# A ring of four pairs of PSUM banks: one pool's choice, or four named buffers in turn

## The chip, the cores and the metric

The kernel runs on one core of one Trainium2 chip. The metric is the device time of one execution in microseconds (us); the kernel before has a median of 836.28 us over 4 runs (833.42 to 839.04). Clock figures are those of TensorE as the profile records them: 1.00 is full speed, 0.50 half.

## The reference

Input x has 4 sequences of 1024 tokens with 256 channels, all in float32. Two residual layers follow each other.

```
x = x + causal_attention(layernorm(x))     # 16 heads of 16, ALiBi slopes, softmax, output projection
x = x + ffn(layernorm(x))                  # below
```

The second layer attends over the 4 sequences at each token position (16 heads, softmax over 4), projects, adds and normalises, and then sends every token to one expert out of 8: the router takes the two best of 8 logits, and the larger index of the two is the expert. The expert is two 256 x 256 matrices with an exact GELU between them; its output is added and normalised again.

## The kernel before

`fast_layer` writes the program out in a fixed order; nothing is reordered afterwards. The attention over 1024 positions is cut into units. A unit is a sequence and a block of queries, 256 of them (units 0 to 11) or 128 (units 12 to 19, the last quarter of the positions). For every unit and each of 4 groups of 4 heads there are rounds over the keys:

- `score` (L950) takes two pairs of PSUM banks (`sk_unit_group_round_0` and `_1`), fills them with matmuls of `slots` with `slots`, lets ScalarE take the exponential of each pair into a `probs` buffer `p` (7 of them), and lets GpSimd cut the diagonal blocks (`affine_select`, L981).
- `weigh` (L987) handles the probabilities two rounds later: it takes one more pair (`pv_unit_group_round`), fills its first bank with matmuls of `p` with the values `v`, and ScalarE or VectorE moves it to `yt`, which goes to DRAM for later normalising (`y<-yt`, L1031).
- Beside these rounds, planned by hand in slots with costs (`E_slot`, `D_slot`), runs everything else: projections of q, k and v (`qkp`, `vp`, copied to `kq` and `v`), the division by the sums of the softmax (`load_sums` L1038, `invert`, `load_y`, `divide`: tiles `sums`, `inverse`, `su`, `yc`), the output projection (`project`, tile `op`, added to `x`), and the second layer's `front` (L1546: `u`, `ut`, `qkvp`, `pr`, `sc`, `ctx`, `ctp`, `ao`, `place`, `rank`).

All of these take their PSUM from one place. PSUM has 8 banks; during the attention all 8 belong to the pool `ps_s` as four pairs. `pair_of_banks` (L658) takes a pair for `score` or `weigh`; `bank` (L662) takes a pair for the other work and gives it out in halves, the second half to the next caller that needs one bank. A second half goes with the pair's name, so in the profile `kq<-op` is a copy out of the second half of a pair whose first half is `op`. A pair is free again when its last reader, a ScalarE or a VectorE instruction, has read it; until then the first matmul into it waits, and all of TensorE's queue behind that matmul.

As each engine executes in order, the time of a wait depends on which pair is next. The pool before is one ring of four buffers under one tag, and the pool chooses which of them a call gets when the program is built. That is nearly always the pair taken four calls ago, and in a few places it is not.

After the attention three single banks (`tail_banks`) and the pool `ps_x` serve the last position block and the expert tiles (`mtp`, `hid`, `oe`), which end with indirect DMAs to the output (L1924).

The engines are called PE (TensorE), PEld (its weight loads), DVE (VectorE), ACT (ScalarE), POOL (GpSimd) and SP (SyncE, which issues most DMAs) in the profile. Nearly all rows have line L584, a helper that records operands, so rows are told apart by their tiles.

Of the kernel before, what the change touches and what calls it, by code (L numbers as in the profile page):

```python
# [29 lines left out]
F32 = mybir.dt.float32  # L30
# [5 lines left out]
PSUM = bass.MemoryType.PSUM  # L36

P = 128
# [6 lines left out]
QC = 512  # L45
# [557 lines left out]
def fast_layer(ctx: ExitStack, tc: tile.TileContext, odd, x, wq, wk, wv, wp, w_in, w_out, w_r,  # L603
# [27 lines left out]
    pool = lambda name, bufs, **k: tc.tile_pool(name=name, bufs=bufs, **k)  # L631
# [7 lines left out]
    attention = ExitStack()  # L639
    pad = attention.enter_context(pool("pad", 1))  # L640
    act = attention.enter_context(pool("act", 1))
    probs = attention.enter_context(pool("probs", N_PROBS))
    ps_s = attention.enter_context(pool("ps_s", 4, space=PSUM))

    def const(name, shape, dtype=F32, into=keep):
        return into.tile(shape, dtype, tag=name, name=name)
# [5 lines left out]

    half_of = []
    tail_banks = []

    def pair_of_banks(name):  # L658
        half_of.clear()
        return ps_s.tile([P, 2, QC], F32, tag="s", name=name)  # L660

    def bank(name):  # L662
        if tail_banks:
            return tail_banks[0].tile([P, QC], F32, tag="m", name=name)
        if half_of:
            return half_of.pop()
        pair = pair_of_banks(name)
        halves[pair.tensor.name] = [], []
        half_of.append(pair[:, 1])
        return pair[:, 0]  # L670
# [279 lines left out]
    def score(u, g, r):  # L950
# [4 lines left out]
        qt = slots[g][:, i * P:(i + size) * P]  # L955
        own = r == n_rounds(u) - 1
        ps = [pair_of_banks(f"sk_{name}_{k}") for k in range(2)]
        width = 0
        for kb, off in blocks_of(u, r):
# [27 lines left out]
    def weigh(rounds_):  # L987
# [4 lines left out]
        for u, g, r, pts in rounds_:  # L992
            if not parts or parts[-1][0] != (u, g):
                parts.append(((u, g), []))
            parts[-1][1].append((r, pts))
        pm = pair_of_banks("pv_{}_{}_{}".format(*rounds_[0][:3]))[:, 0]
        for k, ((u, g), of_part) in enumerate(parts):
            n, i, size = units[u]
# [1325 lines left out]
@with_exitstack  # L2324
def tile_layer(ctx: ExitStack, tc: tile.TileContext, *args):
    nc = tc.nc
    flag = ctx.enter_context(tc.tile_pool(name="flag", bufs=1))
    odd = flag.tile([P, 1], I32, tag="odd", name="odd")
    fast_layer(tc, odd, *args)
    again = nc.values_load(  # L2330
        odd[0:1, 0:1], min_val=0, max_val=1,
        skip_runtime_bounds_check_because="a comparison's result",
    )
    with tc.If(again > 0):
        general_layer(tc, *args)
# [75 lines left out]
```

## Time and profile before

| | us |
|---|---|
| median of 4 runs | 836.28 (833.42 to 839.04) |
| the profiled execution, its own time | 833.63 |
| its span, first to last instruction | 831.9 |
| PE busy | 724.7 (87%) |
| DVE busy | 547.0 (66%) |
| ACT busy | 417.6 (50%) |
| POOL busy | 255.3 (31%) |
| mean granted clock | 0.943 |

The stages by the clock of the span: about 100 us of preparation and first units, attention with the second layer's fronts beside it to about 655 us, the last front and the first expert tiles to about 740 us, then expert tiles to the end. In a timeline row the columns are start, busy time, engine, line, operation, out<-in, shapes, count, and in brackets the idle time before it with what ended it. `pv<-p,v x64` is 64 matmuls of one shape, merged.

### The profile page before, as it was taken

Reading aid. Unit: us, or ns where it says so; the run is one execution under the profiler, and the core shown is the slowest. Engines: PE = TensorE matmul, PEld = TensorE weight load, DVE = VectorE, ACT = ScalarE, POOL = GpSimd, SP = SyncE. Lnnn points to the kernel's source line nnn. Section 1 sums busy time; section 2 is a strip of 40 time slices with the busy share of each in tenths; the row PEclk is TensorE's granted clock in tenths of the full one; section 3 lists DMA queues with packets and bytes.
Section 4 is the critical chain, followed back from the end, with each engine's and each line's share of the span. In section 5 each row is a group of like instructions: output and inputs, shape, how many; then the busy total and the mean of one; then the engine's idle time right before and its main releaser. Section 6 shows DMA issues by size and latency. Waiting matters only on the chain. (4 is left out here: it accounts for less than half of the span.)

```text
span 831.9 us, 22499 instructions
## 1 busy us (share of the span) xinstructions
PE 724.7 (87%) x8917; PEld 542.8 (65%) x8917; DVE 547.0 (66%) x1316; ACT 417.6 (50%) x625; POOL 255.3 (31%) x360
## 2 busy tenths in 40 slices
PE   4987989999899889999989997988988799878972
PEld 2765667666566556665668876767766567767772
DVE  7245336429647957595778748388479779885663
ACT  1554446666455636665456456557445345333540
POOL 5433113212111301121122112112112414648885
PEclk9798989999999989999989999999998899898996
DMA  7444454434522415152444535424421662233430
GB/s 216 118 128 143 130 159 126 144 110 132 153 73 76 126 47 171 54 164 72 123 124 144 149 108 146 126 78 126 145 78 28 208 231 77 71 108 120 128 100 24
DMA packets 75219, 99.56 MB, mean 120 GB/s; under 512 B 19496, under 2 KB 58723, under 8 KB 74596
## 3 DMA queue, kind: packets, MB, share of 16 engines
q1 hardware_dynamic: 64576, 79.63, 32.4%
q0 software_dynamic: 4864, 14.16, 5.6%
q10 hardware_dynamic: 5668, 4.25, 1.7%
q8 instruction: 73, 1.20, 0.6%
q14 instruction: 38, 0.31, 0.1%
HBM read 61.55 MB, written 35.12 MB: 116 GB/s over the span
## 5 line engine op out<-in xcount | busy, mean ns | idle before, releaser
L584 ACT ACTIVATE p<-sk 128x1024 f32<-128x1024 f32 (+1 forms) x320 | 288.4, 939 | 180.1 <-PE sk L584 158.0
L981 POOL TENSOR_SCALAR_AFFINE_SELECT p<-p 128x512 f32<-128x512 f32 (+1 forms) x160 | 106.3, 669 | 447.5 <-ACT p L584 445.1
L584 PE MATMUL sk<-slots 32*128 32x128 f32 (+1 forms) x3456 | 185.7, 332 | 22.6 <-DVE rank L584 6.8
L584 PEld LDWEIGHTS sk<-slots 32*128 32x128 f32 x3456 | 139.7, 191 | 69.6 <-issue 24.5
L584 PE MATMUL pv<-p,v 128*32 128x128 f32 (+1 forms) x3456 | 148.4, 320 | 9.8 <-DVE x L584 3.1
L584 PEld LDWEIGHTS pv<-p,v 128*32 128x32 f32 x3456 | 99.4, 114 | 48.2 <-issue 9.3
L584 PE MATMUL qkvp<-w_in,ut 128*128 128x264 f32 (+1 forms) x236 | 83.2, 486 | 0.0
L584 PEld LDWEIGHTS qkvp<-w_in,ut 128*128 128x128 f32 x236 | 41.2, 190 | 29.1 <-issue 24.8
L584 PE MATMUL oe<-w,ge 128*128 (+1 forms) x152 | 43.8, 413 | 12.9 <-DVE stats_v L584 6.7
L584 DVE COPY qkv<-qkvp 128x264 f32<-128x264 f32 x28 | 12.1, 432 | 61.9 <-PE qkvp L584 61.9
L1808 POOL DMA_INDIRECT given<-rows,rows x38 | 42.8, 1126 | 20.0 <-DVE at_t L584 10.0
L584 PE MATMUL hid<-mt,w 128*128 128x128 f32 x304 | 46.9, 292 | 2.1 <-DMA w<-in_w_dram 1.4
L584 PEld LDWEIGHTS hid<-mt,w 128*128 128x128 f32 x304 | 41.9, 200 | 3.4 <-DMA w<-in_w_dram 1.7
L1924 POOL DMA_INDIRECT out_dram<-o,out_rows x38 | 39.8, 1046 | 8.7 <-issue 5.9
L584 DVE TENSOR_TENSOR pv<-qkv,sc 128x1024 f32<-128x1024 f32 x32 | 40.5, 1267 | 0.3 <-PE ctp L584 0.2
L584 DVE TENSOR_REDUCE sc<-pr 128x64 f32<-128x1024 f32 x32 | 39.0, 1220 | 1.1
L584 DVE TENSOR_TENSOR pr<-qkv 128x1024 f32<-128x1024 f32 x32 | 39.5, 1236 | 0.0
L584 PE MATMUL op<-wp,yc 128*128 128x256 f32 x124 | 33.4, 410 | 7.0 <-issue 3.4
L584 PE MATMUL qkp<-xt,wqk 128*128 128x256 f32 x144 | 38.8, 416 | 0.2 <-ACT p L584 0.2
L584 PEld LDWEIGHTS oe<-w,ge 128*128 128x128 f32 x152 | 27.2, 200 | 17.6 <-DVE given L584 7.5
L584 ACT COPY qkv<-qkvp 128x512 f32<-128x512 f32 (+1 forms) x31 | 17.3, 561 | 40.9 <-PE qkvp L584 40.8
L584 PE MATMUL vp<-wv,xt 128*128 128x256 f32 x128 | 35.0, 421 | 0.0
(320 smaller groups left out, 1053.1 us busy)
## 6 DMA issues: line engine op xcount, KB each, us to landing
slots<-k SPq DMA_DIRECT2D x128, 80.0 KB
k<-kq SPq DMA_DIRECT2D x32, 256.0 KB
v<-v SPq DMA_DIRECT2D x16, 288.0 KB
v<-v SPq DMA_DIRECT2D x4, 1152.0 KB
x<-in_x_dram SPq DMA_DIRECT2D x16, 256.0 KB
y<-yt SPq DMA_DIRECT2D x16, 256.0 KB
rows<-x SPq DMA_DIRECT2D x32, 128.0 KB
slots<-k SPq DMA_DIRECT2D x64, 64.0 KB
```

Of the source, the lines that this page charges most:

```text
L584: ins = made(*args, **kwargs)
L981: nc.gpsimd.affine_select(blocks, blocks, pattern=[[0, 2], [0, size], [1, P]], compare_op=ALU.is_ge, fill=0.0, base=0, channel_multiplier=-1,)
L1808: nc.gpsimd.indirect_dma_start(out=self.hx, out_offset=None, in_=t.rows_of, in_offset=bass.IndirectOffsetOnAxis(ap=t.rows_[:, self.j:self. ...
L1924: ins = nc.gpsimd.indirect_dma_start(out=out.rearrange("t n c -> (t n) c"), out_offset=bass.IndirectOffsetOnAxis(ap=t.table.out_rows[:, t. ...
```

## The change

The pool `ps_s` gets one buffer per tag, and four tags `s0` to `s3`. A counter goes up at each call of `pair_of_banks`, and its remainder by 4 picks the tag. So every call takes the pair that was taken four calls before, whichever was read last.

```diff
-    ps_s = attention.enter_context(pool("ps_s", 4, space=PSUM))
+    ps_s = attention.enter_context(pool("ps_s", 1, space=PSUM))
...
-    half_of = []
+    half_of, n_pairs = [], [0]
     tail_banks = []
 
     def pair_of_banks(name):
         half_of.clear()
-        return ps_s.tile([P, 2, QC], F32, tag="s", name=name)
+        n_pairs[0] += 1
+        return ps_s.tile([P, 2, QC], F32, tag=f"s{n_pairs[0] % 4}", name=name)
```

No computation, shape or order of instructions differs. What differs in the built program is the instruction whose end a TensorE matmul waits for, at six places (the matmul, then the reader of its pair before and after):

```
105 us  pv_4_0_0      turned_w copy (ACT)      -> kq<-op copy (DVE)
        sk_4_2_0_1    kq<-op copy (DVE)        -> p_4_1_1_0 (ACT)
508 us  pv_15_0_0     x<-x,op (DVE)            -> p_15_1_0_1 (ACT)
        sk_15_2_0_0   p_15_1_0_1 (ACT)         -> x<-x,op (DVE)
559 us  sk_17_0_1_1   rank<-place (DVE)        -> p_17_0_0_0 (ACT)
        sk_17_1_0_0   p_17_0_0_1 (ACT)         -> rank<-place (DVE)
567 us  pv_17_0_0     x<-x,op (DVE)            -> p_17_1_0_1 (ACT)
        sk_17_2_0_0   p_17_1_0_1 (ACT)         -> x<-x,op (DVE)
623 us  sk_19_0_1_1   rank<-place (DVE)        -> p_19_0_0_0 (ACT)
        sk_19_1_0_0   p_19_0_0_1 (ACT)         -> rank<-place (DVE)
640 us  pv_19_1_0     yn<-sum (DVE)            -> p_19_2_0_1 (ACT)
        sk_19_3_0_0   p_19_2_0_1 (ACT)         -> yn<-sum (DVE)
```

Three more matmuls beside these (`sk_4_2_0_0`, `pv_16_3_0`, `pv_18_3_0`) change from one ScalarE reader to its neighbour.

## The prediction

> **What bounds the kernel now.** I read the page's busy table and its 40 slices first, then TensorE's waits from 500 to 660 us, then the timeline around each place that the change touches, then a table of stretches for clock and VectorE load. TensorE is busy 724.7 of 831.9 us and fills nearly every slice, so in most of the attention part it sets the time. The list of TensorE's waits (waiting instruction, releaser, total us, times, longest us) shows where it does not:
>
> ```profile
> PE sk L584 <- DVE rank L584: 6.8, 2, 3.4
> PE ctp L584 <- DVE ctx L584: 4.2, 3, 2.0
> PE pv L584 <- DVE x L584: 3.1, 1, 3.1
> PE pv L584 <- DVE yn L584: 2.9, 1, 2.9
> ```
>
> Rows 1, 3 and 4 are waits for a PSUM pair: VectorE's `rank`, `x` and `yn` instructions are no operands of `sk` or `pv`; they are the last readers of the pair that was to be reused. That is 12.75 us in four stalls (3.10, 3.38, 3.38, 2.89). Compared instruction by instruction, the two built programs have the same instructions in the same order on every engine, and differ only in what 15 TensorE instructions wait for. They form six places; in each, two pairs swap their turn, one freed by ScalarE, one by VectorE. Five of the six decide, so each is worked out below. A fifth stall of this kind, at 110.38 us, is made longer.
>
> The second thing to see is what lies beside the stalls. In the table of stretches (us; busy of PE, PEld, DVE, ACT, POOL; granted clock; DMA share; GB/s):
>
> ```profile
> 505.00:508.00 3.00, 0.04 (x4) 0.00 (x0) 2.93 (x8) 1.11 (x2) 0.36 (x1) 0.98 0.85 319
> 508.00:511.30 3.30, 3.15 (x58) 2.58 (x58) 3.16 (x6) 0.81 (x1) 0.31 (x2) 0.50 0.95 291
> 619.60:623.00 3.40, 0.04 (x2) 0.00 (x0) 3.33 (x4) 1.43 (x2) 0.00 (x0) 1.00 0.62 161
> 623.00:627.40 4.40, 4.38 (x90) 3.93 (x92) 4.19 (x10) 2.05 (x2) 1.14 (x2) 0.61 0.01 4
> ```
>
> VectorE is full exactly where TensorE stands still, so a removed stall may only send TensorE to VectorE's next result. And after each such idle time the granted clock is 0.50 for about 3.4 us (0.61 over 4.4 us is 3.4 us at half).
>
> **The price of such a slow spell.** 64 `pv` matmuls take 1.88 us at full clock (566.88 to 568.76), 56 of them take 3.15 at half (508.14 to 511.29), so a factor of 1.92, and a spell of 3.4 us that falls on busy TensorE costs 3.4 x (1 - 1/1.92) = 1.6 us.
>
> ```profile
> 508.14 3.21 PE L584 MATMUL pv<-p,v 128*32 128x128 f32 x56 [3.10 <-DVE x L584]
> ...
> 566.88 1.96 PE L584 MATMUL pv<-p,v 128*32 128x128 f32 x64
> ```
>
> **Part A, unit 4 at 105 us.** Today `pv_4_0_0` takes the pair of `turned_w`, free at 104.86. In strict turn it takes the pair of `op_1`, whose last reader is the copy to `kq`:
>
> ```profile
> 105.03 1.72 PE L584 MATMUL pv<-p,v 128*32 128x256 f32 x32
> 106.68 0.70 PE L584 MATMUL sk<-slots 32*128 32x256 f32 x4
> 109.64 0.68 DVE L584 COPY kq<-op 128x512 f32<-128x512 f32 x1
> 110.38 0.50 PE L584 MATMUL sk<-slots 32*128 32x256 f32 x4 [3.00 <-DVE kq L584]
> ```
>
> The copy is held by `inverse` at the head of VectorE's queue, which waits for the DMA of `sums` until 107.53, so it stays at 110.32. The 3.00 us stall becomes 5.35, and the work that ran ahead of it (pv 1.65, sk 0.70) comes behind it: +2.35. Queued behind the waiting `pv` are all later matmuls, and the exp whose `probs` buffer it frees. The clock now drops only after 111.9; with the idle time from 105.03 on I expect it low already at 110.38, 1.5 us x (1 - 1/1.92) = 0.7 more. A = +3.1, bounds 2.35 (clock unchanged) and 4.0 (a whole spell more). Nothing covers it: TensorE has no idle time over 0.25 us until 192, and VectorE's long busy stretches after that (from 182.7, 262.5, 414.0, 492.9) each begin at a wait that a `qkvp` matmul ends, so they move along.
>
> **Part B, unit 15 at 508 us.** The 3.10 us stall of `pv_15_0_0` goes (its new pair is free at 503.54, its probabilities at 501.66). `sk_15_2_0_0` takes the late pair instead and waits for `x` until 508.09; TensorE is then 3.1 us ahead. But the next thing that it needs is `ctx` at 521.54, where it already waits 0.64 us. VectorE is busy from 492.9 up to there but for 1.68 us at 513.86, spent on the DMA of `sums`, which SP issues behind four stores of rows that wait for VectorE itself. So the gain is nothing, and the idle time in front of 521.6 is 3.7 us, which calls a spell onto the `qkvp` matmuls behind it. B = +1.6, bounds 0 (the spell fell on 508 and is only moved) and +1.6.
>
> **Part C, units 16 and 17 at 559 us.** The 3.38 us stall and its spell go: `pv_16_3_0` ends at 558.8 instead of 563.45 (start 556.9 when its pair is free, 1.88 at full clock). Then `op_15` waits for `yc`, which VectorE finishes at 562.33; 2.2 us are left, and a spell after that idle time leaves about 0.9 at `sk_17_1_1`. The swap at 566.88 has both pairs free before it (566.14 and 566.65) and costs nothing. What ends last here is VectorE, and it has a hole:
>
> ```profile
> 575.61 0.25 DVE L584 RECIPROCAL inverse<-sums 128x16 f32<-128x16 f32 x1 [3.14 <-DMA sums<-y]
> ```
>
> That load is issued at 569.83, lands 5.8 us later behind the 1.15 MB load of `v`, and hangs on TensorE through the store of `yt` (after `pv_16_3_0`) and fills that wait for `sk_17_1_1`. I put the issue at 569.0 and, with `v` out of its way, its landing 3.3 us after that as at 510.55 to 513.84: 572.3, when VectorE gets there at 572.47. C = -3.1. Bounds: -0.8 (only the issue moves) and -4.7 (TensorE's 1.60 and 1.99 us waits for `ctx` at 580.84 and 583.16 shrink too, and with them a spell).
>
> **Part D, units 18 and 19 at 623 and 640 us.** Two stalls go, 3.38 and 2.89, with their spells. VectorE has no wait between 614.94 and 651.10, and TensorE needs `yc` from it twice:
>
> ```profile
> 628.53 0.41 DVE L584 TENSOR_TENSOR yc<-yc,su 128x256 f32<-128x256 f32 x1
> ...
> 650.68 0.42 DVE L584 TENSOR_TENSOR yc<-yc,su 128x256 f32<-128x256 f32 x1
> ...
> 629.05 1.10 PE L584 MATMUL op<-wp,yc 128*128 128x256 f32 x4 [0.27 <-issue]
> ...
> 651.21 1.10 PE L584 MATMUL op<-wp,yc 128*128 128x256 f32 x4 [0.54 <-ACT yt L584]
> ```
>
> `op_17` can start 0.1 us earlier and `op_18` 0.06 us: both gains are gone there. About 3.3 us of new idle time before 651.2 put a spell on `op_18` and the first sums, 1.54 us that VectorE waits for: 1.54 x 0.92 = +1.4. D = +1.4, bounds -0.1 and +1.6.
>
> **Sum.** 3.1 + 1.6 - 3.1 + 1.4 = +3.0 us. The profiled execution took 833.63 us (span 831.9), 2.65 under the median of the four runs, 836.28; its own time becomes 836.6, the median 839.3. The lower bounds together give -2.5, the upper +6.4.
>
> The Trainium skill ("TensorE: Matmul & The Clock Gate", Part 1, and the section on HAM oscillation) has the clock halved after an idle window of about 3.4 us of a free-running counter, and advises against idle gaps longer than that. Read strictly it leaves the four stalls of 2.89 to 3.38 us free of charge, and this trace disagrees: 0.50 follows the one of 3.10 us. By the rule only the 5.35 us of part A would pay, B and D would be near 0, and the sum would be about 0; I take the row. The rule speaks against this change all the same, since it joins small idle times into longer ones.
>
> **The rivals.**
> - Faster: every removed stall counts. -12.75 + 3.1 = -9.65 us, 826.6; with four spells of 1.6 less, 820.2. For it: TensorE is the busiest engine and these are its longest waits in this part. Against it: VectorE's busy 2.93 of 3.00 and 3.33 of 3.40 us during two of them. It decides when over 7.3 us of the 12.75 reach the end, which needs VectorE to wait for TensorE somewhere between 614.94 and 651.10.
> - Slower by over 0.5%: part C pays only its lower bound, because `sums` lands as late behind `v` as now. 3.1 + 1.6 - 0.8 + 1.4 = +5.3, 841.6. It decides once the hole at 575.61 shrinks by less than 1.9 us. For it: the fills ahead of `sums` move by only about 0.9.
> - The swap does nothing: A sinks into the 5.61 us that TensorE waits for `xn` at 294.82, and all else into VectorE. 836.2. Against it: VectorE's stretch before `xn` begins at a `qkvp` matmul.
>
> **How the numbers follow.** A measurement of this kernel tells about 0.5% (4.2 us) from no change. The forecast case, ending within that bound, has 0.44, the third rival 0.14: within 0.5% 0.58. The slower rival has 0.32, the faster 0.10. The range, 833.5 to 843.5, takes in the bounds of the sum from the low side (836.28 - 2.5) to the slow one (+6.4) and 0.5 to 1 us for where the clock's spells fall; it leaves out the faster rival and the far end of the slower one.
>
> **What would show it.** In the profile after: one TensorE wait of about 5.3 us for `kq` at 110 us; the rows `sk <- rank`, `pv <- x` and `pv <- yn` gone; a wait for `ctx` near 521 of over 2 us instead of 0.64; `op` waiting for `yc` in units 17 and 19; the hole before `inverse` at 575 smaller. I am wrong if TensorE is still ahead at 652 us by more than the shift it carried in at 615, if the lag of A is gone before 500, or if the clock stays at full after the new idle times.

## The result and the profile after

The change makes the kernel very slightly faster: a median of 835.46 us (44 runs, 831.14 to 839.78) against 836.74 us for the kernel before (70 runs, 829.90 to 842.08), a ratio of 0.9986 with a 95% interval of 0.9976 to 0.9996, or -1.2 us. That is within the 0.5% that was given the largest chance, and inside the range, but on the other side of no change than the forecast of +3.0 us. Repeated in two later groups of runs the same program gave -2.8 us (0.9966, 0.9934 to 0.9998) and -1.4 us (0.9983, 0.9960 to 1.0006).

The profiled execution took 834.87 us (span 833.2, mean granted clock 0.943). The pair of profiled executions shows +1.2 us, the medians -1.2: the profile of before came from an execution 3.1 us below the median of its 70 runs. A sum made on one execution carries such an offset, and below it turns out to be larger than most terms of the sum.

The list of TensorE's waits from 500 to 660 us, of the kernel after (waiting instruction, releaser, total us, times, longest us):

```profile
PE ctp L584 <- DVE ctx L584: 6.2, 4, 2.0
PE op L584 <- issue: 5.0, 1, 5.0
PE op L584 <- ACT p L584: 3.4, 2, 2.0
PE pv L584 <- DVE who_f L584: 1.7, 1, 1.7
PE sk L584 <- DVE x L584: 1.4, 1, 1.4
```

The rows `sk <- rank`, `pv <- x` and `pv <- yn`, 12.75 us together, are gone. In their place TensorE waits for what VectorE makes: `ctx` (6.2 instead of 4.2), `op` for `yc` (the rows "issue" and "ACT p"; the 4.97 us of the first end 0.1 us after VectorE's `yc`), and twice a pair: `sk_15_2_0_0`, which has taken the late pair at 508 us, for `x`, and the last `pv` of unit 19 for `who_f`. At the first of the six places (place 1, part A) the timeline of the kernel after reads:

```profile
104.54 0.94 PE L584 MATMUL sk<-slots 32*128 32x256 f32 x16
110.84 3.21 PE L584 MATMUL pv<-p,v 128*32 128x256 f32 x32 [5.36 <-DVE kq L584]
113.98 2.09 PE L584 MATMUL sk<-slots 32*128 32x256 f32 x16
116.00 2.36 PE L584 MATMUL vp<-wv,xt 128*128 128x256 f32 x8
```

The wait is the 5.35 us of the forecast. `vp`, which took 3.33 us before, takes 2.36: the granted clock is 0.50 until 116.7 us and 1.00 behind that. The hole of VectorE before `inverse` in unit 17, 3.14 us before, has closed, and the one in unit 15 has grown from 1.68 to 2.95 (VectorE's timeline of the kernel after; the second row has no bracket, so no idle time):

```profile
516.56 0.25 DVE L584 RECIPROCAL inverse<-sums 128x16 f32<-128x16 f32 x1 [2.95 <-DMA sums<-y]
...
577.34 0.24 DVE L584 RECIPROCAL inverse<-sums 128x16 f32<-128x16 f32 x1
```

Where the pair of profiles parts is seen by comparing the start of the same VectorE instruction in both. Positive is a longer stretch after:

| stretch of before, us | parts in it | after minus before, us |
|---|---|---|
| 0 to 99 | none | +0.38 |
| 99 to 131 | A | +1.24 |
| 131 to 500 | none | -0.10 |
| 500 to 541 | B | +3.70 |
| 541 to 592 | C | -4.37 |
| 592 to 672 | D | +0.29 |
| 672 to the end | none | +0.10 |

### The profile page after: what moved, and what is told of

It is laid out like the page before. It is cut to its first block, busy times and chain, and to the rows that moved or that the text cites. A ratio compares the mean times of both kernels' runs of the same rounds, so it can differ in the third digit from the quotient of the medians.

```text
span 833.2 us, 22499 instructions
## 1 busy us (share of the span) xinstructions
PE 721.3 (87%) x8917; PEld 537.9 (65%) x8917; DVE 545.5 (65%) x1316; ACT 417.3 (50%) x625; POOL 253.6 (30%) x360
## 5 line engine op out<-in xcount | busy, mean ns | idle before, releaser
L584 PE MATMUL pv<-p,v 128*32 128x128 f32 (+1 forms) x3456 | 145.6, 316 | 10.7 <-DVE kq L584 6.6
L584 PEld LDWEIGHTS pv<-p,v 128*32 128x32 f32 x3456 | 96.6, 111 | 49.1 <-issue 9.3
L584 PE MATMUL qkvp<-w_in,ut 128*128 128x264 f32 (+1 forms) x236 | 85.5, 497 | 0.0
L584 PE MATMUL op<-wp,yc 128*128 128x256 f32 x124 | 35.2, 427 | 14.2 <-issue 8.1
L584 PEld LDWEIGHTS op<-wp,yc 128*128 128x128 f32 x124 | 24.1, 207 | 21.9 <-issue 11.6
```

Source lines behind the costliest of these rows:

```text
L584: ins = made(*args, **kwargs)
```

## The experiments

**How the kernels are made.** The ring of the kernel before can be written as four named buffers with seven exceptions, counted in calls of `pair_of_banks`; with all seven the waits are those of before, with none those of the change. Each experiment keeps some of them, and nothing else differs:

```diff
+    ring, out_of_turn = [0, 1, 2, 3], {65: 1, 66: 1, 405: 1, 448: 2, 455: 1, 499: 2, 512: 1}
...
+        ring.append(ring.pop(out_of_turn.get(n_pairs[0], 0)))
+        n_pairs[0] += 1
+        return ps_s.tile([P, 2, QC], F32, tag=f"s{ring[-1]}", name=name)
```

65 and 66 are part A, 405 is B, 448 and 455 are C, 499 and 512 are D; a part whose numbers are absent is strict. All comparisons have 12 runs against 29 to 35 of before in the same group. An interval reaches some 2 to 3 us to either side, so one comparison tells apart only large terms. The first four were meant to test the forecast's terms: A +3.1, B +1.6, C -3.1, D +1.4.

**e1, part A alone.**

```diff
-    out_of_turn = {65: 1, 66: 1, 405: 1, 448: 2, 455: 1, 499: 2, 512: 1}
+    out_of_turn = {405: 1, 448: 2, 455: 1, 499: 2, 512: 1}
```

> Strict turn at the first place only (unit 4, 105 us); at the five others the pairs are taken as before. The forecast's terms: part A alone, +3.1 us (bounds 2.35 and 4.0). The terms as one pair of profiles (before, after) shows them, from the shift of equal instructions between 95 and 490 us: +1.1 us. The rival that the lag sinks into the 5.61 us wait for xn at 295 us: 0. In the profile all three expect one TensorE wait of about 5.3 us for kq at 110 us; the forecast and the profile pair expect the xn wait to keep its 5.6 us, the rival expects it shorter by the lag.

Measured: 1.0004 (0.9975 to 1.0033), +0.3 us. The forecast's +3.1 (a ratio of 1.0037) lies outside.

**e2, part B alone** (405 taken out).

> Strict turn at the second place only (unit 15, 508 us). The forecast's terms: part B alone, +1.6 us, because TensorE's gain ends at the ctx of 521 us, which does not move, and a half-speed spell follows the longer idle time there. The profile pair: +3.7 us, because VectorE's hole before the inverse at 514 us also grows (1.68 to 2.95 us) and the spell is two windows (6.8 us) long. The rival that removed stalls count: -3.1 us or less.

Measured: 1.0040 (1.0014 to 1.0067), +3.3 us: twice the forecast, which the interval (+1.2 to +5.6) still holds.

**e3, part C alone** (448 and 455 taken out).

> Strict turn at the third and fourth place only (units 16 and 17, 559 to 569 us). The forecast's terms: part C alone, -3.1 us (bounds -0.8 and -4.7), through VectorE's 3.14 us hole before the inverse at 575 us. The profile pair: -4.1 us, the hole closed and no half-speed spell at 583 us. The slower rival: -0.8, the hole stays. The rival that removed stalls count: -3.4 and a spell of 1.6, -5.0.

Measured: 0.9942 (0.9916 to 0.9969), -4.9 us: the sign of the forecast, just past its far bound of -4.7, and faster than both kernels.

**e4, part D alone** (499 and 512 taken out).

> Strict turn at the fifth and sixth place only (units 18 and 19, 623 and 640 us). The forecast's terms: part D alone, +1.4 us, by a half-speed spell after 651 us. The profile pair: -0.2 us, no spell there, since pv of unit 19 waits 1.66 us for VectorE at 649 us and the idle time comes in pieces. The rival that removed stalls count: -6.3 us and spells.

Measured: 1.0043 (1.0021 to 1.0064), +3.6 us. The four add up to +2.3, the whole change had given -1.2. In e4's timeline something is seen that no other kernel had shown so far:

```profile
648.44 2.40 PE L584 MATMUL pv<-p,v 128*32 128x128 f32 x64 [2.01 <-DVE who_f L584]
655.04 2.07 PE L584 MATMUL op<-wp,yc 128*128 128x256 f32 x4 [4.20 <-ACT yt L584]
```

The copy `yt` between the two starts at 654.73, 3.9 us after the modelled end of `pv_19_3`. The semaphore that tells of the end of that product was raised only at 654.70, 3.86 us after the modelled end, and the granted clock is 0.50 from 654.9 on, as it is after idle times elsewhere. So TensorE very likely stood still, and this is called the stop below. The semaphores that the product's later matmuls wait for had all been raised before its first one started at 648.44.

**e5, B, C and D** (only 65 and 66 kept).

> The strict turn everywhere but at place 1, where the old order stays (parts B, C and D without A). The terms of the forecast: 1.6 - 3.1 + 1.4 = -0.1 us against the kernel before, so the whole change (-1.2) would have to be 3.1 us slower than this. The sum of the parts run singly: 3.3 - 4.9 + 3.6 = +2.0. The stretches of the profiles from 99 to 131 us say that A costs almost nothing (the two kernels with A are +0.40 and +1.24 there, the four without it 0, +0.57, +0.77 and +0.98, so +0.2 in the mean): this kernel then is at -1.4, within 0.5 us of the whole change.

Measured: 1.0021 (0.9994 to 1.0048), +1.8 us, with the stop (3.98 us).

**e6, C and D** (65, 66 and 405 kept).

> The strict turn only at places 3 to 6 (parts C and D). Additive from the parts run singly: -4.9 + 3.6 = -1.3 us. If the cost of D alone is the 3.9 us that TensorE stood still inside pv_18_3 in that one kernel, and goes when the units before it run at another time, it is C and the +0.3 that the stretch from 615 to 672 us lost in the profile of the whole change: -4.6. The terms of the forecast give -3.1 + 1.4 = -1.7.

Measured: 0.9985 (0.9959 to 1.0012), -1.3 us, with the stop (4.01 us). That is the sum of C and D, so in these runs D's cost did not hang on the units before it.

**e7, A, B and C** (499 and 512 kept).

> The strict turn at places 1 to 4, the old order at places 5 and 6 (parts A, B and C). Additive from the parts run singly: 0.3 + 3.3 - 4.9 = -1.3 us, so D would add nothing to the whole (-1.2) where alone it cost 3.6. If D costs 3.6 inside the whole too, this kernel is at -4.8. The terms of the forecast give 3.1 + 1.6 - 3.1 = +1.6. In its profile the stretch from 500 to 540 us should be about 3.6 longer and the one from 555 to 592 about 4.4 shorter than before.

Measured: 0.9989 (0.9966 to 1.0012), -0.9 us. Its stretches were not the expected +3.6 and -4.4 but +1.45 and -2.76: B and C come in two sizes with nearly the same sum, which is explained below.

**e8, C, and at place 1 the late pair put off further.**

```diff
+    out_of_turn = {65: 1, 66: 1, 67: 1, 68: 1, 405: 1, 499: 2, 512: 1}
```

> A version made from the findings: the strict turn at places 3 and 4 only (part C), and at place 1 the pair that VectorE reads late is put off by two more turns, so that sk_4_2_0_1 takes a pair that ScalarE has freed and the router matmuls take the late one. If waits for a late pair are what place 1 costs, the 3.00 us stall for kq goes, TensorE runs 16 sk and half of vp earlier and then waits for xn, which VectorE makes after kq; the stretch from 99 to 131 us becomes 1 to 3 us shorter than in the kernels with the old order there, and the whole is at -6 to -8 against -4.9 for part C alone. If VectorE and the load of yc set the end of that stretch, it is no shorter and the whole stays at -4.9.

Measured: 0.9940 (0.9912 to 0.9967), -5.0 us, the same as C alone. Place 1 was 0.7 us shorter than before, less than the scatter of that stretch (from -1.5 to +1.4 in the kernels with the old order there). The stall for `kq` did go: TensorE's idle time in the stretch is 1.45 us instead of 3.79, but 10.2 us of its work fall at half clock instead of 6.8. The fast version is C; the stall at 110 us is not worth a wait moved.

**e9, the whole change again** (no exceptions; the built program is the one of the change).

> The whole change once more (the strict turn at all six places), beside the partial versions on the same chip. If the parts simply add, the four run singly make 0.3 + 3.3 - 4.9 + 3.6 = +2.3 us against the kernel before, and the -1.2 measured first does not return. If the whole is really -1.2, then A takes 3.0 us off where B, C and D are strict (B, C and D together measured +1.8), and the 4 us stop of TensorE inside pv_19_3, which all three kernels with D but without A show (3.86, 3.98 and 4.01 us), is again missing here. The forecast's terms: +3.0.

Measured: 0.9966 (0.9934 to 0.9998), -2.8 us, no stop.

**e10, A, B and D.** The expectation speaks of A and D, but 405 is absent as well, so B is strict too.

```diff
+    out_of_turn = {448: 2, 455: 1}
```

> The strict turn at places 1, 5 and 6 only (parts A and D). If the parts add: 0.3 + 3.6 = +3.9 us, with the 4 us stop of TensorE in pv_19_3. If A takes away what D costs: 3.6 - 3.0 = +0.6, without the stop, and the stretch from 615 to 672 us as long as before. The forecast's terms: 3.1 + 1.4 = +4.5.

Measured: 1.0032 (1.0003 to 1.0061), +2.7 us, no stop: for A, B and D the terms without a stop make 0.3 + 3.3 + 0 = +3.6, with it +7.2.

**e11, part B with TensorE kept busy.** In front of the third and fourth `ctx` operand of unit 15:

```diff
                 for t in range(B):
+                    for _ in range(14 if name == "ct" and i == 4 and cc == 0 and t > 1 else 0):
+                        nc.tensor.transpose(pt[:, t * P:(t + 1) * P], ident, ident)
                     nc.tensor.transpose(
```

> The strict turn at place 2 only (part B, +3.3 us), and in the two waits of 1.99 us for ctx at 519 and 521 us TensorE gets 14 more transposes each of the constant ident, written to a PSUM region that the true transposes overwrite (nothing is left out). They fill most of the idle time and change nothing else. If the half clock on the qkvp matmuls behind it (1.92 and 2.92 us instead of 1.02 and 1.91 at full clock) is 1.9 us of part B, and the 1.3 that VectorE's longer wait for sums at 514 us costs the rest, the stretch from 500 to 541 us falls from +3.5 to about +1.5 and the whole to about +1.4. If the clock is not what makes B cost, the stretch stays at +3.5 and the whole at +3.3.

Measured: 0.9999 (0.9970 to 1.0029), -0.1 us; the stretch from 500 to 541 us fell from +3.50 to +0.83. The timeline, first of e2, then of e11:

```profile
519.26 0.33 PE L584 MATMUL ctp<-ident,ctx 128*128 128x128 f32 x1 [1.99 <-DVE ctx L584]
521.59 1.33 PE L584 MATMUL ctp<-ident,ctx 128*128 128x128 f32 x5 [1.99 <-DVE ctx L584]
522.71 1.92 PE L584 MATMUL qkvp<-w_in,ut 128*128 128x512 f32 x2
```

```profile
517.59 1.69 PE L584 MATMUL ctp<-ident 128*128 128x128 f32 x14
519.74 0.33 PE L584 MATMUL ctp<-ident,ctx 128*128 128x128 f32 x1 [0.46 <-DVE ctx L584]
519.91 1.69 PE L584 MATMUL ctp<-ident 128*128 128x128 f32 x14
522.06 0.76 PE L584 MATMUL ctp<-ident,ctx 128*128 128x128 f32 x5 [0.46 <-DVE ctx L584]
522.66 1.02 PE L584 MATMUL qkvp<-w_in,ut 128*128 128x512 f32 x2
```

`ctx` is as late as before, 2.3 us apart, but idle times of 1.99 us have become 0.46, and `qkvp` behind them takes 1.02 us instead of 1.92. The granted clock is 1.00 all through that stretch in e11, while VectorE's hole at 514 us is as large as in e2 (2.92 and 3.10 us). So the half clock is the larger part of B, some 2.7 of the 3.5 us in this pair of profiles.

**e12, A and D.**

```diff
+    out_of_turn = {405: 1, 448: 2, 455: 1}
```

> The strict turn at places 1, 5 and 6, the old order at 2, 3 and 4 (parts A and D; in the kernel meant for this before, place 2 was strict as well, so that one held A, B and D). If the parts add: 0.3 + 3.6 = +3.9 us, with the 4 us stop of TensorE in pv_19_3 (three kernels with D and without A have it: 3.86, 3.98, 4.01). If A takes the stop away, as in the three kernels that hold both: about +0.3, without the stop, and the stretch from 615 to 672 us within 1 us of before.

Measured: 0.9997 (0.9975 to 1.0018), -0.3 us, no stop.

**e13, D alone in other physical banks; e14, the whole change in the banks of D alone.**

```diff
+    out_of_turn = {65: 1, 66: 1, 209: 1, 211: 1, 405: 1, 448: 2, 455: 1}     # e13
+    out_of_turn = {206: 1, 208: 1}                                           # e14
```

> Part D alone, and in unit 9 (near 270 us) two pairs change places in the ring, where all four are free early. Nothing waits for that, but from there on every tile lies in the same physical banks as in the whole change, while the waits at places 1 to 4 stay the old ones. If the stop in pv_19_3 hangs on which banks are used, it is gone and the time is within 0.5 us of before. If it hangs on something else that A does, the stop of 4 us is there and the time is +3.6 us, as for D alone.

Measured: 1.0029 (1.0005 to 1.0053), +2.4 us, but no stop in its profile, whose execution (834.55 us) was the second fastest of the 12.

> The converse: the strict turn at all six places, and two pairs change places in unit 9 so that from there on the tiles lie in the physical banks of part D alone. If the banks decide, the 4 us stop in pv_19_3 appears and the time is 3.6 above that of the whole change (-1.2 and -2.8 were measured), so +0.8 to +2.4. If they do not, the time stays at -1.2 to -2.8 and there is no stop.

Measured: 0.9987 (0.9966 to 1.0009), -1.1 us, no stop. The exchanged banks brought no stop to e14 and no loss of time; e13 can't say whether other banks take the stop away, since D alone in its own banks has none either off the chip of e4 (e16 below). Why e13 was slow in the median is open.

**e15, a version that beats both: the whole change with the 28 transposes of e11.**

> A version made from the findings: the whole change, and the 2 x 14 transposes of the constant ident in front of the two late ctx operands of unit 15, which took part B from +3.3 to -0.1 us. The stretch from 500 to 541 us should be +0.8 instead of +3.65 against before and the whole 2.8 to 3.4 us faster than the whole change: -4.0 to -6.2 us against the kernel before. If the time won there is lost again at the next wait for VectorE, it stays at -1.2 to -2.8.

Measured: 0.9958 (0.9938 to 0.9978), -3.5 us; its stretch from 500 to 541 us was -0.20 against before where the change has +3.70. The expectation's near end was missed by half a microsecond. In the same group the median was 832.22 us, against 835.24 of e14, the change with two pairs exchanged. Part C alone (e3, e8) stays the fastest that was run; a kernel with C and the transposes wasn't tried.

By now the kernels with the stop had all run on one chip, those with D and without it on others. So three were repeated.

**e16, D alone again; e17, the whole change again; e18, B, C and D again** (the programs of e4, e9 and e5).

> Part D alone once more. The kernels that showed the 4 us stop in pv_19_3 (D; C and D; B, C and D) had all run on one chip, those with D and without the stop on others, so the chip has to be told apart from part A. If the stop belongs to D without A, it is there again and the time is +3.6 us against the kernel before. If it belongs to that chip or to those runs, D alone has no stop elsewhere and its time is between 0 and +1.5 (the stretch from 615 to 672 us between +0.2 and +0.9, as in the kernels with D and without the stop).

Measured: 0.9999 (0.9973 to 1.0024), -0.1 us, no stop.

> The whole change a third time, on the chip of the two others of this group: -1.2, -2.8 and (with two pairs exchanged) -1.1 us were measured against the kernel before, so -1 to -3. If this chip gives D its stop whatever A does, there is a stop here as well and the time is +1 to +3.

Measured: 0.9983 (0.9960 to 1.0006), -1.4 us, no stop.

> Parts B, C and D without A once more, which measured +1.8 us with the stop. If D without A brings the stop: +1.8 again, and 3 us above the whole change of this group. If not: B and C give 3.6 - 4.35 = -0.75 in the profiles, D about +0.3, so about -0.5, within 1 us of the whole change.

Measured: 0.9979 (0.9958 to 1.0001), -1.8 us, no stop.

The two rows of e4 above read so in e16, the same program:

```profile
651.51 1.95 PE L584 MATMUL pv<-p,v 128*32 128x128 f32 x64 [2.01 <-DVE who_f L584]
654.52 1.10 PE L584 MATMUL op<-wp,yc 128*128 128x256 f32 x4 [1.05 <-ACT yt L584]
```

So the theory that A takes D's cost away falls: D costs nothing that these runs can show where there is no stop, and the stop of 3.9 to 4.0 us appeared in all three profiles with D from one chip, and in none of the ten other profiles with D (nine from three other chips; the record doesn't name the chip of the first pair). Without it the parts add again: 0.3 + 3.3 - 4.9 - 0.1 = -1.4 us for the whole change, measured -1.2, -2.8 and -1.4.

## Why the prediction was wrong

**What moves the terms from run to run.** The clock records of all 20 profiles show one pattern. The full clock gives way to half only at edges of a grid of 3.413 us, whose position differs from execution to execution and is the same to within 0.003 us inside one. Over the 3360 grid windows at full clock between 60 and 700 us, the clock of the next window goes with TensorE's idle time in this one as follows:

| idle time in the window | next at half | next at full |
|---|---|---|
| under 1.3 us | 9 | 3069 |
| 1.3 to 1.65 us | 8 | 63 |
| 1.65 to 2.0 us | 30 | 15 |
| over 2.0 us | 166 | 0 |

A half window (a grid window at clock 0.50) is followed by another when over 0.9 us of it was idle (100 of 100), and by full speed when under 0.5 us was (208 of 220). An idle time of 2 to 3 us is thus cheap or dear according to where the grid cuts it. The Trainium skill ("TensorE: Matmul & The Clock Gate", Part 1) has the free-running counter of about 3.4 us, and these records agree; it has the clock halved after an idle window, where here 2.0 us of idle time in the window were enough every time.

**Part A, +3.1 forecast, +0.4 found.** This is the step that failed most: "Nothing covers it", and 0.7 more for a spell, both taken from one execution. The stretch from 99 to 131 us against before is +0.37 us in the mean of nine profiles with the strict order there (-0.37 to +1.24) and -0.02 in the mean of ten with the old one (-1.46 to +1.42), so A costs 0.4 us, give or take 0.4. The longer wait for `kq` came as forecast: 4.4 us in the mean of the nine, 2.0 in the mean of the ten, so +2.4 where +2.35 was said. But half of it is covered by a later product, `op` at 122 us, which needs `yc` from VectorE. `yc` is done 22.4 us into the stretch in the mean of the nine and 22.5 in that of the ten, so the longer wait doesn't move it. First before, then e5, which has the old order at place 1:

```profile
121.53 0.81 DVE L584 TENSOR_TENSOR yc<-yc,su 128x512 f32<-128x512 f32 x1 [3.34 <-DMA slots<-k]
122.83 1.99 PE L584 MATMUL op<-wp,yc 128*128 128x256 f32 x8
```

```profile
122.06 0.69 DVE L584 TENSOR_TENSOR yc<-yc,su 128x512 f32<-128x512 f32 x1 [4.42 <-DMA slots<-k]
122.85 1.97 PE L584 MATMUL op<-wp,yc 128*128 128x256 f32 x8 [2.12 <-ACT p L584]
```

The profile names `p`, but `op` starts 0.10 us after `yc` is done, in e5 and in all the six of the ten that wait here (0.96 to 2.81 us). In the mean of the ten this wait is 1.2 us; in none of the nine is there any, since TensorE now comes later than `yc`. The profile of before doesn't show the wait because its half window from 118.8 to 122.2 us fell on the work in front of `op`, which so came 0.5 us after `yc`. TensorE's idle time in the stretch is therefore 5.2 against 3.9 us, +1.3 (2.4 less 1.2) and not +2.35. Busy time at half clock is 6.05 against 6.09 us, so in the mean the spell of the forecast isn't there; and some 0.7 us of work go because the `sk` matmuls are no longer cut in two (0.70 and 1.13 us before, 1.15 in one piece at full clock).

**Part B, +1.6 forecast, +3.0 found.** That is the mean of nine profiles with the strict order here and without the transposes (+1.4 to +3.8); nine with the old order are within 0.15 us of before. The gain was nothing, as said: TensorE's new lead ended in two waits for `ctx`. Two sizes were off. The spell had two windows instead of one in six of the nine profiles, and `sums` came later. A table of stretches of the kernel after:

```profile
519.60:521.60 2.00, 0.06 (x1) 0.00 (x0) 1.93 (x4) 1.30 (x2) 0.00 (x0) 1.00 0.06 19
522.00:525.00 3.00, 1.03 (x5) 1.03 (x6) 1.85 (x3) 0.51 (x1) 0.00 (x0) 0.66 0.50 148
525.00:530.30 5.30, 5.30 (x15) 2.49 (x13) 0.69 (x1) 0.66 (x2) 0.00 (x0) 0.55 0.07 15
```

TensorE is idle while VectorE is full (1.93 of 2.00 us), and the 5.3 us of `qkvp` that follow run at 0.55. VectorE's hole at 514 us, which the forecast left as it was, grew by 1.3 us, since the load of `sums` was issued 0.7 us later against the shift at that place and took 0.5 longer. Both are seen in e2 too (hole 3.10 us). Where the grid gave one half window instead of two (e7, e14, e17), the hole was 1.8, 1.8 and 2.4 us and the stretch +1.4 to +1.8, near the forecast. The prediction's remark that the rule leaves B near 0 doesn't fit its own 3.7 us of idle time, which is over 3.4; the idle time then came in two pieces of 1.99 us.

**Part C, -3.1 forecast, -4.7 found.** That is the mean of eleven profiles with the strict order here (-4.4 to -2.8) less that of nine with the old one (-0.35 to +1.96, mean +0.8): the old order comes in two sizes too, and the profile of before has the short one. The mechanism held: the hole before `inverse` is gone in all eleven and 2.8 to 3.4 us long in all nine, and half clock fell with it (e3: 6.25 us of it on busy TensorE between 500 and 592 us, 9.79 before). B and C share what the grid does: their sum is -0.55 to -1.38 us in seven profiles with both, -0.9 in the mean, and the six with neither are at +0.3, so -1.2 together; the forecast had -1.5. That this came so near is luck: both terms were too small by about the same amount.

**Part D, +1.4 forecast, about -0.6 found.** The two gains were gone at `op_17` and `op_18`, as said; TensorE waits 4.97 us for `yc` at 630.13. But the spell that was to hit `op_18` needed 3.3 us of idle time in one piece. They came as 1.66 us (`pv_19_3` for `who_f`) and 1.05 us on either side of 1.95 us of work, so no window of 3.41 us holds more than 1.66 us of them. Of ten profiles with D and no stop only e17 has a half window there (650.7 us), and its stretch from 615 to 672 us is the longest, +1.25; the ten have +0.11 in the mean, seven without D +0.74, so -0.6, give or take 0.4. From 615 to 652 us nine of the ten have two half windows, both beginning in the wait that ends at 630 us, where the seven have two to four.

**The sum.** 0.4 - 1.2 - 0.6 = -1.4 us, where -1.2, -2.8 and -1.4 were measured (each of the three terms is uncertain by about 0.4), against 3.1 + 1.6 - 3.1 + 1.4 = +3.0. Of the 4.4 us between the two sums, 2.7 are A's and 2.0 are D's. Of the signs by which the forecast was to be judged, the wait for `kq` (5.36), the rows gone, `ctx` over 2 us, the wait in unit 17 and the smaller hole all came; `op_18` waited 1.05 us for `yt`, not for `yc`; TensorE was not ahead at 652, and A's lag of +1.5 was still there at 500 in that one profile. It named the new waits rightly; it missed the wait that covers A, and it mispriced the idle time.

The rival "every removed stall counts" is refuted by the waits that took the stalls' place. "The swap does nothing" gave the nearest number (836.2) by luck: the wait for `xn` at 296.39 us kept its 5.61 us, so A does not sink there but in part at `op` at 122 us, and C isn't nothing. "Part C pays only its lower bound" is refuted by e3.

## What to carry to other kernels

A wait for a buffer removed in front of a full engine becomes a wait for that engine's result: find what the waiting engine needs next, and look for a hole of the other engine that its lead can fill, as part C did and A, B and D did not. An idle time of TensorE is priced by the half clock behind it, and that by how it is cut into windows, so a few cheap matmuls on a constant in front of a late operand (e15 against e14: 3.0 us between the medians) can be worth as much as the order of the buffers. Before writing "nothing covers it", look for the next product that needs a late result even where the profile shows no wait there: a half window can hide it. A sum of terms under 2 us read from one execution is within the noise of that execution: measure the same stretch in several before giving it a sign.

## What the runs showed of the hardware

- The granted clock of TensorE changes on a grid of 3.413 us with one position per execution, and over 2.0 us of idle time in a window was followed by a half window in all 166 cases counted here.
- On one of the four chips of the experiments one product (`pv_19_3`) ended 3.86, 3.98 and 4.01 us later than modelled, beside the first indirect gathers of GpSimd, whose fifth was late as well (1.3 to 1.5 us instead of 0.30). The starts of its matmuls become uneven 1.44 us after the first, in all three profiles. Three kernels without D ended the same product 1.07 to 1.09 us late on that chip, two others 0.35 and 0.37. No semaphore seen in the traces explains it; in two of the three a 16 KB load of instructions landed 0.14 and 0.25 us before the end of the stop, in the third none did. The cause is open.
